# Graph attention and a graph convolution on one core: the second batch's keys and values as block products, and six scalings ahead of a rectification

## The chip, the core and the metric

The kernel runs on one core of a Trainium2 chip. The metric is device time in microseconds (us), smaller is better. The kernel before took 2423.48 us, the median of three runs (2422.51 to 2423.66).

A core has five engines that run side by side and wait for each other by semaphores: TensorE (PE, matrix products into PSUM; its weight loads are listed as PEld), VectorE (DVE), ScalarE (ACT), GpSimd (POOL) and SyncE (SP, which here issues most DMAs). PSUM holds eight banks of 128 x 512 floats.

## The reference, cut to what matters

x is 16 x 1024 x 256 (batch, node, channel), adj is 1024 x 1024, all in float32. Two layers, each with a residual and a layernorm:

```
# layer 0: attention with graph-mixed queries
fea = x^T;  c_adj = mean over channels
Wg = adj * (1 - |2*sigmoid(c_adj[m]-c_adj[n]) - 1|), symmetrised   # per batch
q  = relu((fea @ Wg) * para)          # 4 heads of 64
k, v = split(x @ kv_w)                # kv_w: 256 x 512
x = layernorm(x + softmax(q k^T * scale) v)
# layer 1: A_hat = normalised adj
h = relu(batchnorm((A_hat @ x) @ W1^T + b1));  o = batchnorm(h @ W2^T + b2)
x = layernorm(x + o)
```

## The kernel before

All of this concerns `fast_path`. Layer 0 works one batch at a time, 16 batches in a row. For a batch b there are 32 *units* (two pairs of heads, two halves of the queries, eight blocks of 128 keys). A unit is a call of `scores` (L1152: keys times queries into a two-bank PSUM tile `ps`, then the exponential on ACT, L1157, into a tile `p`) and a call of `outputs` (L1173: `p` times the values into `po`; DVE adds the `p` of a group into `acc`, L1181 and L1183). There are two `ps` tiles and four `p` tiles. Units are issued in 16 bursts of two, numbered u = 0 to 15: scores of burst u, then outputs of burst u-1.

Between the bursts of batch b, the next batch's preparation and the end of the batch before are threaded in. The order of every instruction on PE, ACT, DVE and SP is written out by hand (`tc.manual_schedule`); an engine takes its instructions strictly in the order of the program text. POOL is left to the order of its calls. The pieces that matter here:

- `prologue(b)` makes the closures of a batch's preparation: `begin` (channel sums on DVE, L812, and the row `crow`), the transposes of x, the weights `wg` (ACT: abs L840 and tanh L845; DVE: times adj, L849), the queries, the keys and values.
- Batch 0's queries are plain products (`graph_first`, L979, then `queries`, L966 and L969). For the other batches q is seven block products of a 2 x 2 blocking with sums of blocks on either side (seven products instead of eight): `p1` to `p7` (L899). p1, p2 and p3 run in burst 4 of the batch before, p6, p7, p5 and p4 in burst 8. p2 ends in DVE's product with para (L930) and ACT's rectification (L909); p3 ends in an ACT copy (L926).
- Keys and values of batches 0 and 1 are plain products: `keys` (L994) and `values` (L1007), four steps each. Batches 2 to 15 have them as seven block products too: `kv_step` for k = 1, 6, 5, 7, 3, 4 in burst 0 of the batch before, and `kv_last` (k = 2) in burst 4, between p1 and p2. Each product has a part for the keys (L1054, 512 columns) and one for the values (L1057, four times 128 columns). DVE prepares four sums of blocks of x (`kv_sum`, L1049) and adds each product in (L1066); ACT copies the first (L1074). POOL prepares sums of the weights once (`kv_weight_sums`, L756 to L759), partly over the weights themselves, so after the last plain product has read them.
- The layernorm of batch b-1 (`moments_x1`, `apply_x1`) is threaded into bursts 2 to 5 of batch b, for b = 1 to 14. ACT takes the sums (L1286, L1290), POOL makes the coefficients (L1296 to L1300), ACT scales the eight blocks of 256 columns (L1305), and behind the eighth it issues the DMA that stores x (L1310). In burst 4 ACT's order is: second moments, four scalings, the rectification of p2, the copy of p3. In burst 5: two exponentials, four scalings, the store. SP then loads the x of batch b+2 into the tile that the store frees (L770), a batch that DVE's channel sums in burst 8 read.

The head of the program prepares batch 0 and then batch 1: `graph_first(0..7)` with pieces of batch 1's weights in between, then batch 1's four `values` and four `keys` steps, then the first scores.

After layer 0 come the graph products of layer 1 (L1733), two linear layers with batchnorm (L1765, L1942) and the last residual and layernorm (L2078 to L2167); nothing of them is touched.

Of the kernel before, what the change touches and what calls it, by code (L numbers as in the profile page):

```python
# [515 lines left out]
def fast_path(  # L516
# [23 lines left out]
    NCH = N // P  # L540
# [184 lines left out]
    graph = ExitStack()  # L725
# [9 lines left out]
    with (  # L735
# [17 lines left out]
        def kv_weight_sums():  # L753
            (a11, a12), (a21, a22) = kvA
            s2, s3, s4 = (kvS[:, i] for i in range(3))
            nc.gpsimd.tensor_tensor(s3, a11, a21, ALU.subtract)  # L756
            nc.gpsimd.tensor_tensor(a21, a21, a22, ALU.add)
            nc.gpsimd.tensor_tensor(s2, a21, a11, ALU.subtract)
            nc.gpsimd.tensor_tensor(s4, a12, s2, ALU.subtract)  # L759

        st = {}

        def load_x(b):
            t = xp.tile([P, NCH, C], F32, tag="x", name=f"x_{b}")
            src = x[b].rearrange("(n p) c -> p n c", p=P)
            if b == 0:
                for n in range(0, NCH, 4):
                    nc.sync.dma_start(t[:, n : n + 4, :], src[:, n : n + 4, :])
            else:
                nc.sync.dma_start(t, src)  # L770
            st[b] = {"x": t}

        def load_squares(b, c):
            xs = st[b]["xS", c] = xsp.tile([P, N // SQ, SQ], F32, tag="xS", name=f"xS_{b}_{c}")
            src = x[b].rearrange("(j k) (c q i) -> c q k j i", k=SQ, q=NQ, i=SQ)
            for q in range(NQ):
                nc.sync.dma_start(xs[q * SQ : (q + 1) * SQ], src[c, q])
# [20 lines left out]
        def prologue(b):  # L798
# [6 lines left out]
            def step(f, *a):  # L805
                steps.append((f, a))
# [212 lines left out]
            kv = {}  # L1019
# [85 lines left out]
            else:  # L1105
                first.append((begin, ()))
                first += [(transpose_squares, (c,)) for c in range(CC)]
            for i in range(4 if b < 2 else 0):
                step(values, i)
                step(keys, i // 2, i % 2)  # L1110
            for n in range(NCH if b == 0 else 0):
# [15 lines left out]
            if b:  # L1127
                s["graph"] = dict(
                    between=between, p=(None, p1, p2, p3, p4, p5, p6, p7), right=right, left_first=left_first,
                    kv=(kv_tiles, kv_sum, kv_step, kv_last), q_tile=q_tile,  # L1130
# [186 lines left out]
        def run(fs, k):  # L1317
            for f, a in fs[:k]:
                f(*a)
            del fs[:k]  # L1320
# [135 lines left out]
        with tc.manual_schedule(  # L1456
# [10 lines left out]
            next_first, next_steps, next_side = prologue(1)  # L1467
            for i in range(8):
# [3 lines left out]
                if i == 6:  # L1472
                    run(next_first, 1)
                    load_squares(1, 0)
            run(side, 99)
            for n in range(NCH):
                run(steps, 1)
                if n in (1, 5):
                    run(next_first, 1)
                if n == 1:  # L1480
                    load_squares(1, 1)
                if n:
                    run(next_side, 3)
            for _ in range(8):
                run(next_steps, 1)
                run(next_side, 1)
            kv_weight_sums()
            full, sums, late = [], [], []
            rows_of = []

            def back(j):

                for i in bursts[j]:
                    outputs(i)
                b, pr, qh, m = units[bursts[j][-1]]
                if m == NCH - 1 and qh == 1:
                    sums.append((normalise, (b, pr)))
                    for q in range(2):
                        full.append((residual, (b, pr, q)))
                    if pr == PAIRS - 1:  # L1500
                        if b < B - 2:
                            lo, hi = range(NCH // 2), range(NCH // 2, NCH)
                            late.extend(
                                [(moments_x1, (b, k, ns)) for k in (1, 2) for ns in (lo, hi)]
                                + [(apply_x1, (b, ns)) for ns in (lo, hi)]
                            )

            last, before_last = {}, {}
# [16 lines left out]
            for i in range(4):  # L1525
                ns = range(2 * i, 2 * i + 2)
# [4 lines left out]
            for j in range(len(bursts)):  # L1531
                b, u = j // PERB, j % PERB
                outputs_first = j and u == 0 and b < B - 1
                if outputs_first:
                    back(j - 1)
                for i in bursts[j]:
                    scores(i)
                if u == 0:
                    steps, side = next_steps, next_side
                    next_first, next_steps, next_side = [], [], []  # L1540
                if j and not outputs_first:
                    back(j - 1)
                if outputs_first:
                    run(sums, 1)
                if u in (5, 9, 13):
                    run(rows_of, 1)
                if u == 5:
                    run(late, 1)
                if u == 5 and b + 2 < B:
                    load_x(b + 2)  # L1550
                    next_first, next_steps, next_side = prologue(b + 2)
                if b == B - 1:
                    if u == 0:
                        run(sums, 1)
                        run(rows_of, 1)
                    elif u in (2, 13):
                        run(full, 2)
                    elif u == 8:
                        run(sums, 1)
                    elif u == 3:  # L1560
                        late.clear()
                elif u == 0:
                    if b == 0:
                        run(rows_of, 1)
                        run(side, 99)
                    else:
                        tiles, total, product, kv_last = st[b + 1]["graph"]["kv"]
                        tiles()
                        total(2)
                        for i, k in enumerate((1, 6, 5, 7, 3, 4)):  # L1570
                            if i == 0:
                                run(side, 1)
                            product(k, 0)
                            product(k, 1)
                            if i == 0:
                                run(rows_of, 1)
                                run(side, 1)
                                total(3)
                            run(side, (1, 2, 2, 2, 1, 0)[i])
                            if i == 2:  # L1580
                                total(4)
                elif u < 4:
                    if u == 1:
                        run(full, 2)
                    run(side, (None, 1, 2, 3)[u])
                    if u == 3:
                        st[b + 1]["graph"]["left_first"]()
                    if u > 1:
                        run(late, 1)
                elif u == 4:  # L1590
                    gr = st[b + 1]["graph"]
                    p = gr["p"]
                    run(late, 1)
                    p[1]()
                    if b:
                        run(kv_last(), 2)
                    gr["right"](1)
                    run(late, 2)
                    p[2]()
                    p[3]()  # L1600
                elif u == 8:
                    gr = st[b + 1]["graph"]
                    p = gr["p"]
                    p[6]()
                    run(next_first, 1)
                    run(sums, 1)
                    if b == B - 2:
                        adjacency_diagonal()
                        for n in range(6):
                            adjacency_rows(n)  # L1610
                    p[7]()
                    gr["right"](4)
                    p[5]()
                    p[4]()
                elif u < 8:
                    st[b + 1]["graph"]["between"](u)
                else:
                    if u == 9 and b + 2 < B:
                        load_squares(b + 2, 0)
                    if u == 11:  # L1620
                        run(full, 2)
                    if u == 12:
                        run(next_first, 1)
                        if b + 2 < B:
                            load_squares(b + 2, 1)
                    if u == 15:
                        run(next_first, 1)
                    run(next_side, 2 if u == 11 else 1)
                    if u == 14 and b + 2 < B:
                        st[b + 2]["graph"]["kv"][1](1)  # L1630
                if b == B - 2:
                    run(before_last.get(u, []), 9)
                if b == B - 1:
                    run(last.get(u, []), 9)
# [603 lines left out]
```

## Time and profile before

| what | value |
|---|---|
| median of three runs | 2423.48 us |
| the profiled execution | 2424.15 us |
| its span, first to last instruction | 2422.4 us |
| granted TensorE clock, mean | 0.996 |
| first scores of batch 0 | 65.6 us |
| one batch of layer 0, batches 1 to 14 | some 95.4 us |
| busy in one such batch: PE, DVE, ACT, POOL | 94.8, 87.2, 67.1, 11.2 us |
| last scores of layer 0 | 1541 us |

The profile is one execution taken by the hardware profiler. Its page lists the busy time of each engine, and the groups of instructions by line. The list of waits says for each line how long its engine stood still before it, and which instruction released it. The timeline of an engine gives start, duration, line, operation, output <- inputs, shape, and in brackets the idle time just before with its releaser; equal neighbours are merged ("x16" is sixteen records, and the duration covers all of them). A matrix product in float32 leaves two records per operation. The ends of PE's records are modelled, and neighbours overlap in it; so the starts of PE's rows are the better measure.

### The profile page before, as it was taken

The numbers are of one execution on the slowest core, as the hardware profiler recorded it, in microseconds if no ns is written. First come the engines' busy times: TensorE is split into PE (matmuls) and PEld (weight loads), VectorE is DVE, ScalarE is ACT, GpSimd is POOL, SyncE is SP. The second block draws the span as 40 slices with busy tenths as digits, with TensorE's granted clock in tenths as the row PEclk, the third lists the DMA queues.
The fourth block names the chain that finished last, engine by engine and source line by source line (L and its number), as shares of the span: only waits on it lengthen the run. The fifth ranks groups of instructions, "written<-read, shape, count | busy, mean of one in ns | idle before, by whom it ended". The sixth has DMA issues, their size and how long they took to land. (4 is left out here: it accounts for less than half of the span.)

```text
span 2422.4 us, 33863 instructions
## 1 busy us (share of the span) xinstructions
PE 2378.9 (98%) x12602; PEld 1014.3 (42%) x12602; DVE 1924.7 (79%) x2757; ACT 1323.7 (55%) x1931; POOL 358.2 (15%) x429
## 2 busy tenths in 40 slices
PE   9999999999999999999999999999999999999996
PEld 5343443443434434434434343344444444444444
DVE  5698999989989989899899898955454454479878
ACT  7386776866866867768658677411011011045468
POOL 1011011010110110111101102421111111010026
PEclk9999999999999999999999999999999999999998
DMA  5124222232242242332422426232122122165558
GB/s 165 40 41 88 58 49 71 54 71 65 38 88 58 45 86 55 54 71 42 83 61 41 84 49 112 69 105 104 70 87 104 70 87 104 55 236 178 174 199 358
DMA packets 437886, 222.06 MB, mean 92 GB/s; under 512 B 361552, under 2 KB 411216, under 8 KB 431568
## 3 DMA queue, kind: packets, MB, share of 16 engines
q1 hardware_dynamic: 418400, 169.20, 28.3%
q0 software_dynamic: 2528, 33.57, 3.3%
q10 hardware_dynamic: 16784, 17.04, 2.1%
q8 instruction: 101, 1.65, 0.3%
q14 instruction: 73, 0.60, 0.1%
HBM read 136.06 MB, written 83.69 MB: 91 GB/s over the span
## 5 line engine op out<-in xcount | busy, mean ns | idle before, releaser
L1157 ACT ACTIVATE p<-ps 128x1024 f32<-128x1024 f32 x512 | 497.2, 1021 | 114.8 <-PE ps L1152 95.5
L1183 DVE TENSOR_TENSOR acc<-acc,p 128x1024 f32<-128x1024 f32 x384 | 495.6, 1291 | 35.9 <-ACT p L1157 13.7
L1152 PE MATMUL ps<-qT,kT 64*64 64x512 f32 x4096 | 489.6, 593 | 9.2 <-ACT p L1157 9.2
L1173 PE MATMUL po<-p,v 64*64 64x512 f32 x4096 | 482.8, 589 | 0.0
L1173 PEld LDWEIGHTS po<-p,v 64*64 64x64 f32 x4096 | 158.2, 133 | 281.2 <-issue 278.2
L1152 PEld LDWEIGHTS ps<-qT,kT 64*64 64x64 f32 x4096 | 147.4, 132 | 301.0 <-issue 202.0
L1259 POOL TENSOR_TENSOR o<-o,r_all 128x512 f32<-128x512 f32 x34 | 65.7, 1949 | 638.1 <-DVE r_all L1243 597.2
L849 DVE SCALAR_TENSOR_TENSOR wg<-wg,adj_s 128x1024 f32<-128x1024 f32 x128 | 151.4, 1214 | 3.8 <-ACT wg L845 3.8
L840 ACT ACTIVATE wg<-crow,ccol 128x1024 f32<-128x1024 f32 x128 | 146.4, 1144 | 0.1
L845 ACT ACTIVATE wg<-wg 128x1024 f32<-128x1024 f32 x128 | 135.6, 1060 | 2.2
L909 ACT ACTIVATE qT<-qT 128x512 f32<-128x512 f32 x60 | 37.4, 630 | 168.8 <-DVE qT L912 145.3
L648 DVE SCALAR_TENSOR_TENSOR u_h<-b_h,col_b,p_h 128x512 f32<-128x512 f32 x60 | 45.1, 751 | 98.7 <-PE b_h L1765 98.7
L899 PE MATMUL pgb<-wg,S 128*128 128x512 f32 x240 | 111.0, 605 | 0.0
L899 PE MATMUL pga<-wg,x 128*128 128x512 f32 x240 | 109.6, 599 | 0.7 <-ACT qT L921 0.7
L1733 PE MATMUL a_agg<-ahT,x1l 128*128 128x512 f32 x240 | 108.1, 593 | 0.7 <-ACT agg L1444 0.7
L1733 PE MATMUL b_agg<-aT,x1S 128*128 128x512 f32 x240 | 107.9, 592 | 0.0
L656 ACT COPY p_h<-a_h 128x512 f32<-128x512 f32 x30 | 17.6, 585 | 164.6 <-PE a_h L1765 163.5
L669 ACT ACTIVATE hw<-a_h,col_b 128x512 f32<-128x512 f32 x30 | 20.6, 687 | 132.0 <-PE a_h L1765 132.0
L656 ACT COPY p_agg<-a_agg 128x512 f32<-128x512 f32 x15 | 8.8, 586 | 141.7 <-PE a_agg L1733 141.7
L1296 POOL TENSOR_SCALAR mm_l<-mm_l 128x4 f32<-128x4 f32 x28 | 12.2, 435 | 490.6 <-ACT qT L1286 490.6
L1181 DVE TENSOR_TENSOR acc<-p,p 128x1024 f32<-128x1024 f32 x64 | 77.4, 1210 | 7.5 <-ACT p L1157 7.5
L1305 ACT ACTIVATE x<-x,mm_l 128x256 f32<-128x256 f32 x112 | 58.0, 595 | 44.6 <-POOL mm_l L1300 44.6
(286 smaller groups left out, 3897.9 us busy)
## 6 DMA issues: line engine op xcount, KB each, us to landing
h<-hw POOLq DMA_DIRECT2D x16, 2048.0 KB, 6.6
hl<-h SPq DMA_DIRECT2D x32, 1024.0 KB
x<-x ACTq DMA_DIRECT2D x16, 1024.0 KB
x1l<-x SPq DMA_DIRECT2D x16, 1024.0 KB
xf<-x SPq DMA_DIRECT2D x16, 1024.0 KB
o<-oS SPq DMA_DIRECT2D x62, 256.0 KB
o<-o SPq DMA_DIRECT2D x248, 64.0 KB
x<-in_x_dram SPq DMA_DIRECT2D x15, 1024.0 KB
```

What stands on the lines that cost most here:

```text
L840: nc.scalar.activation(w, s["crow"], AF.Abs, bias=s["ccol"][:, n : n + 1])
L845: nc.scalar.activation(w, w, AF.Tanh, scale=0.5)
L849: nc.vector.scalar_tensor_tensor(w, w, 1.0, adj_s[:, n, :], op0=ALU.subtract, op1=ALU.mult)
L899: nc.tensor.matmul(ps, left, right, start=(start and i == 0), stop=(i == NCH // 2 - 1), skip_group_check=True,)
L1152: nc.tensor.matmul(ps[kh * D : (kh + 1) * D, hd * HALF : (hd + 1) * HALF], kT[r, pr, ks], qT[r, pr, qh * HALF : (qh + 1) * HALF], start=Tr ...
L1157: nc.scalar.activation(p, ps, AF.Exp)
L1173: nc.tensor.matmul(g["po"][kh][hd * D : (hd + 1) * D, :], s["v"][r, m, h * D : (h + 1) * D], p[r, hd * HALF : (hd + 1) * HALF], start=(m = ...
L1181: nc.vector.tensor_add(g["acc"], g.pop("p0"), p)
L1183: nc.vector.tensor_add(g["acc"], g["acc"], p)
L1259: nc.gpsimd.tensor_tensor(oh, oh, r, ALU.mult)
L1305: nc.scalar.activation(s["x"][:, n, :], s["x"][:, n, :], AF.Identity, bias=s["mm"][:, 3, n : n + 1], scale=s["mm"][:, 2, n : n + 1],)
L1733: nc.tensor.matmul(ps, left, right, start=(start and i == 0), stop=(i == NCH // 2 - 1), skip_group_check=True,)
```

## The change

It has two edits.

First, batch 1's keys and values become seven block products as well. In the head, the weight sums are called before batch 0's graph products instead of after batch 1's keys and values. The first two sums of blocks of x go behind batch 1's second transpose, and six products, with the other two sums and what remains of batch 1's weights between them, stand where the eight steps of keys and values stood. The seventh product goes into burst 4 of batch 0, as it does in the other batches.

Second, the eight scalings of a layernorm are divided six and two instead of four and four: six in burst 4, ahead of p2's rectification, and two in burst 5, behind the exponentials.

```
-            for i in range(4 if b < 2 else 0):
+            for i in range(0 if b else 4):
                 step(values, i)
                 step(keys, i // 2, i % 2)
...
             run(side, 99)
+            kv_weight_sums()
+            tiles, total, product, kv_last = st[1]["graph"]["kv"]
             for n in range(NCH):
                 run(steps, 1)
                 if n in (1, 5):
                     run(next_first, 1)
+                if n == 5:
+                    total(1)
+                    total(2)
                 if n == 1:
                     load_squares(1, 1)
                 if n:
                     run(next_side, 3)
-            for _ in range(8):
-                run(next_steps, 1)
+            tiles()
+            for k in (1, 6, 5, 7, 3, 4):
+                product(k, 0)
+                product(k, 1)
+                if k == 1:
+                    total(3)
+                elif k == 5:
+                    total(4)
                 run(next_side, 1)
-            kv_weight_sums()
             full, sums, late = [], [], []
...
                             late.extend(
                                 [(moments_x1, (b, k, ns)) for k in (1, 2) for ns in (lo, hi)]
-                                + [(apply_x1, (b, ns)) for ns in (lo, hi)]
+                                + [(apply_x1, (b, ns)) for ns in (range(6), range(6, NCH))]
                             )
...
                 elif u == 4:
                     gr = st[b + 1]["graph"]
-                    p = gr["p"]
+                    p, kv_last = gr["p"], gr["kv"][3]
                     run(late, 1)
                     p[1]()
-                    if b:
-                        run(kv_last(), 2)
+                    run(kv_last(), 2)
                     gr["right"](1)
                     run(late, 2)
                     p[2]()
```

In the code `total` is `kv_sum`, `product` is `kv_step` with its second argument 0 for keys and 1 for values, and `run(fs, k)` calls the next k closures of a list.

More of the change, by code (lines that the diff above doesn't have):

```diff
@@ L1107, in prologue @@
                 first += [(transpose_squares, (c,)) for c in range(CC)]
-            for i in range(4 if b < 2 else 0):
+            for i in range(0 if b else 4):
                 step(values, i)
@@ L1475, in fast_path @@
             run(side, 99)
+            kv_weight_sums()
+            tiles, total, product, kv_last = st[1]["graph"]["kv"]
             for n in range(NCH):
@@ L1479, in fast_path @@
                     run(next_first, 1)
+                if n == 5:
+                    total(1)
+                    total(2)
                 if n == 1:
@@ L1483, in fast_path @@
                     run(next_side, 3)
-            for _ in range(8):
-                run(next_steps, 1)
+            tiles()
+            for k in (1, 6, 5, 7, 3, 4):
+                product(k, 0)
+                product(k, 1)
+                if k == 1:
+                    total(3)
+                elif k == 5:
+                    total(4)
                 run(next_side, 1)
-            kv_weight_sums()
             full, sums, late = [], [], []
@@ L1504, in back @@
                                 [(moments_x1, (b, k, ns)) for k in (1, 2) for ns in (lo, hi)]
-                                + [(apply_x1, (b, ns)) for ns in (lo, hi)]
+                                + [(apply_x1, (b, ns)) for ns in (range(6), range(6, NCH))]
                             )
@@ L1591, in fast_path @@
                     gr = st[b + 1]["graph"]
-                    p = gr["p"]
+                    p, kv_last = gr["p"], gr["kv"][3]
                     run(late, 1)
                     p[1]()
-                    if b:
-                        run(kv_last(), 2)
+                    run(kv_last(), 2)
                     gr["right"](1)
```

## The prediction

> **What bounds the kernel now.** The page's first part comes first: how full is each engine?
>
> ```profile
> PE 2378.9 (98%) x12602; PEld 1014.3 (42%) x12602; DVE 1924.7 (79%) x2757; ACT 1323.7 (55%) x1931; POOL 358.2 (15%) x429
> ```
>
> PE is busy for 98% of the span, so the time falls only where PE has less to issue or stops waiting. The list of waits, cut to PE, says where it waits. The columns are total us, times, longest:
>
> ```profile
> PE ps L1152 <- ACT p L1157: 9.2, 15, 0.7
> PE pf L2078 <- DVE xf L2106: 7.7, 13, 0.7
> PE pxT L826 <- DMA x<-in_x_dram: 5.0, 1, 5.0
> ```
>
> The first row lies in the attention stage: scores wait until an exponential has read their PSUM tile. The change works there. Batches 1 to 14 have one such wait each, 0.58 to 0.66 us, always in the eighth burst (u = 7); the fifteenth, 0.28, is at the start. Now the timeline of PE in batch 6, from burst 5 on:
>
> ```profile
> 760.44 1.95 PE L1152 MATMUL ps<-qT,kT 64*64 64x512 f32 x16
> 762.21 1.90 PE L1173 MATMUL po<-p,v 64*64 64x512 f32 x16
> 763.92 1.90 PE L1152 MATMUL ps<-qT,kT 64*64 64x512 f32 x16
> 765.64 1.90 PE L1173 MATMUL po<-p,v 64*64 64x512 f32 x16
> 768.20 2.00 PE L1152 MATMUL ps<-qT,kT 64*64 64x512 f32 x16 [0.66 <-ACT p L1157]
> 770.02 1.90 PE L1173 MATMUL po<-p,v 64*64 64x512 f32 x16
> ```
>
> Starts are 1.72 us apart except around the wait, where 2.56 and 1.82 stand. From the first row to the next product p6 (775.28) it is 14.84 us. Batch 0 has no layernorm before it and needs 13.90 for the same stretch (93.23 to 107.13). The wait thus costs 0.94 us, not the 0.66 in brackets. ACT in the same window tells why:
>
> ```profile
> 758.29 2.08 ACT L1305 ACTIVATE x<-x,mm_l 128x256 f32<-128x256 f32 x4 [3.19 <-POOL mm_l L1300]
> 761.73 0.63 ACT L909 ACTIVATE qT<-qT 128x512 f32<-128x512 f32 x1 [1.36 <-DVE qT L930]
> 762.27 0.57 ACT L926 COPY qT<-pgd 128x512 f32<-128x512 f32 x1
> 762.73 1.94 ACT L1157 ACTIVATE p<-ps 128x1024 f32<-128x1024 f32 x2
> 764.55 2.07 ACT L1305 ACTIVATE x<-x,mm_l 128x256 f32<-128x256 f32 x4
> 766.65 0.37 ACTq L1310 DMA_DIRECT2D x<-x  x1
> 767.12 1.94 ACT L1157 ACTIVATE p<-ps 128x1024 f32<-128x1024 f32 x2 [0.50 <-ACT x L1305]
> ```
>
> Four scalings run ahead of q's rectification (L909), and then ACT idles 1.36 us for DVE's product (L930). Four more run behind the exponentials of burst 5, then the store's issue, and only then the exponentials of burst 6. The first of those ends at 768.14, and PE starts at 768.20.
>
> **The scalings, part by part.** Four scalings take 2.08 us at 0.595 each, so starts are 0.495 apart. Six from 758.29 end at 758.29 + 2.08 + 0.99 = 761.36. L930 runs 761.01 to 761.70, so the two added ones fit into the idle 1.36 with 0.34 to spare, and rectification, copy and exponentials keep their places. That idle time is 1.35 or 1.36 in all 14 batches. The cover is ACT's idle time alone; without it (further down) PE's margin is 0.17, since the first exponential of burst 5 ends at 763.75 and scores need its tile at 763.92.
>
> Behind the exponentials 0.99 goes. The store issues at 765.66 and the exponentials start at 767.12 - 0.99 = 766.13; the first ends at 767.15 and frees PE at 767.21. PE wants the tile at 765.64 + 1.72 = 767.36, the second tile at 768.22 against 768.13. The wait disappears, with 0.15 and 0.09 to spare.
>
> What is late next? DVE, without a pause from burst 1 on, idles 1.42 before p6's sum in burst 8 (1.07 in one batch, with 0.46 just before it); it keeps 0.5 if PE comes 0.94 earlier. The four p buffers: the second exponential of burst 8 would wait some 0.1 for DVE's sum, with nothing close behind it. The load of x issued behind the store (771.52 on SP's queue) moves 0.99 earlier too, its reader 0.94. So the whole 0.94 should be kept. Batches 1 to 3 lose 0.89 each, the other eleven 0.94: 2.7 + 10.3 = **13.0 us less**.
>
> **Second batch's keys and values.** Today four value and four key steps stand ahead of the first scores, 32 full-width records of 0.43: 51.58 (first pv) to 65.61 (first scores) is 14.03. PE's rows of batch 6 give the replacement:
>
> ```profile
> 751.73 1.02 PE L1054 MATMUL kve<-xT,kvw_s 128*128 128x512 f32 x2
> 752.59 1.05 PE L1057 MATMUL kve<-kvw_s,xT 128*128 128x128 f32 x8
> 753.48 3.60 PE L899 MATMUL pga<-wg,x 128*128 128x512 f32 x8
> ...
> 819.06 1.12 PE L1054 MATMUL kva<-xT,kvw_s 128*128 128x512 f32 x2
> ```
>
> One product for keys and values is 0.86 + 0.89 = 1.75. Six in a row, as in u = 0 of batch 6, last 10.71 (819.06 to 829.77). Ahead of the first scores that would be 3.3 less. DVE won't allow it. Its order there becomes: four rectification products, wg, a sum, two adds, wg, two adds, a sum, wg, six adds. Durations: adds and sums 0.69 (starts 0.6 apart), wg 1.22. The first add waits for ACT's copy of the first product, behind a tanh and an abs (54.06 + 1.17): copy done 55.78. From there: adds 55.84 and 56.44, wg to 58.26, adds to 59.5, sum to 60.1, wg to 61.2, product 7's adds 61.8 and 62.4, product 3's 63.0 and 63.6. PE must wait for product 5's add before accumulating product 3 (58.7 becomes 58.96) and for product 7's before product 4 (60.7 becomes 61.86). It then ends at 63.6; first scores at 63.7, **1.9 less**. Bounds: 3.3 less where DVE keeps up; 0.4 less where its chain is 1.5 longer. I take 1.9, from the rows.
>
> The seventh product goes into burst 4 of batch 0, between p1 and p2. There p2 now waits 0.68 for ACT's copy (p1 81.79, p2 86.17: 4.38). With a product between, as in batch 6, it is 3.54 + 1.75 = 5.29: **0.9 more**. Its two adds on DVE lie before L930, which idles 3.56.
>
> POOL's three weight sums (0.72 each) come from 65 to about 23.5 to 26, beside DVE's csum reduction (2.28) that the second wg waits for, and that PE waits for. The nearest rows are at odds: two sums L1183 beside POOL took 4.05 instead of 2.55, a transpose L1202 beside POOL's L1260 0.71 as ever. At the first ratio the reduction grows 1.3. I take 0, because it has a single SBUF input like the transpose and the slowed sum has two; 1.3 stays as an end. The two sums put ahead of the queries delay DVE from 50.06 to about 50.15: 0.1. Net of this part: -1.9 + 0.9 = **-1.0**, from -2.4 to +1.8 (0.4 less, 0.9 and 1.3 more).
>
> The Trainium skill's page "TensorE: Matmul & The Clock Gate" (section "Back-to-back issue gap") speaks against block products: in a stream of weight loads and 128-column matmuls it gives about 81 ns each, against about 56 isolated. As an estimate from that ratio, 1.46 x 0.86 would make a value half 1.25, +0.4 each, +2.7 for seven, and the time 2412.2. The trace disagrees, 0.89 for the eight 128-column records against 0.86 for two of 512 columns, and decides.
>
> **Sum.** The profiled execution took 2424.15 (span 2422.4 and 1.75 around it): 2424.15 - 13.0 - 1.0 = 2410.2. The three runs' median, 2423.48, is 0.67 lower: **2409.5 us**.
>
> **Rivals.**
> - Part of the wait stays or turns up elsewhere: margins are 0.09 to 0.15 at the scores and 0.5 at DVE. If half survives: 2423.48 - 6.5 - 1.0 = 2416.0. For it: thin margins. Against: they hold in all 14 batches. Chance 0.16.
> - No gain: DVE, pause-free from burst 1 to 8, is the real bound, or the wait has another cause. 2422.5. Against: DVE idles 1.42 before p6's sum, and PE starts 0.06 after the exponential's end. Chance 0.08.
> - Slower: the six scalings hold up the rectification. If they end d later than L930, the exponentials, scores and all behind them are d late. The 0.94 goes, and each batch is slower than before from about d = 0.85 on, that is 0.34 + 0.85 = 1.2 us above my row. At d = 1.6, 14 x 0.75 - 1.0 gives 2433. Even unoverlapped scalings (0.595 apart) reach only d = 0.26. Chance 0.03.
> - Weight loads bound the 128-column products, 1.25 for a value half: 14.0 - 2.7 saved, 2412.2. The rows refute it: chance 0.01.
>
> The forecast has the remaining 0.72, at 2407 to 2412. The range reaches through half of the first rival: **2406.5 to 2416.5**. Faster by over 0.2% (4.8 us, about what a measurement here can tell from none): 0.72 + 0.16 + 0.01 = 0.89; within it 0.08; slower 0.03.
>
> **What would show it.** PE's list of waits: ps on ACT falls from 15 times and 9.2 us to one or two. ACT: L1305 as six, then two, with L909 still released by DVE's L930 some 0.35 after the sixth. Burst 5 to p6 is 13.9 in batches 1 to 14, the batch 94.5 instead of 95.4. First scores near 63.7, and p1 to p2 in batch 0 5.3. I am wrong if L909 comes right behind the sixth scaling, if PE waits at burst 6's scores, or if DVE's idle time before p6's sum is gone and PE waits for DVE.

## The result, and the profile after

The changed kernel takes 2409.16 us, the median of four runs (2409.01 to 2409.73), against 2423.57 for the kernel before (four runs, 2422.51 to 2423.85). The ratio is 0.9942, with a 95% interval of 0.9925 to 0.9959: 14.4 us less, where 14.0 was forecast. The profiled execution took 2409.73 with a span of 2407.9, 14.5 less than before.

The page's line of busy times, which answers to the first one shown of before:

```profile
PE 2372.7 (99%) x12624; PEld 1015.8 (42%) x12624; DVE 1932.6 (80%) x2771; ACT 1322.4 (55%) x1927; POOL 358.9 (15%) x429
```

PE is busy 6.2 us less in a span that is 14.5 shorter. The rest is time in which it stood still. Not all of the 6.2 is work saved, either: each wait before has 0.28 us that the profile counts as busy (last section), 3.9 us in 14 batches. The waits of PE (total us, times, longest), cut to those that answer to before and the two new ones in the head:

```profile
PE pf L2087 <- DVE xf L2115: 7.7, 13, 0.7
PE pxT L826 <- DMA x<-in_x_dram: 5.0, 1, 5.0
...
PE kvd L1054 <- DVE kT L1066: 0.9, 1, 0.9
...
PE kvc L1054 <- DVE kT L1066: 0.4, 1, 0.4
PE ps L1152 <- ACT p L1157: 0.3, 1, 0.3
```

Scores on exponentials have gone from 15 waits and 9.2 us to one of 0.3, the one at the start. The two waits of block products on DVE's adds are those that the prediction worked out for the head.

First, a label. With batches counted from 0, the stretch at 760 us that the prediction and the expectations call batch 6 lies in batch 7: its wait is the seventh of the fourteen, and the first is batch 1's. The six products at 819 us lie in burst 0 of batch 8. The stretch is called batch 7 from here on. PE in batch 7, from burst 5 on (start, duration, line):

```profile
754.49 1.04 PE L1152 MATMUL ps<-qT,kT 64*64 64x512 f32 x8
755.35 1.90 PE L1173 MATMUL po<-p,v 64*64 64x512 f32 x16
757.07 1.90 PE L1152 MATMUL ps<-qT,kT 64*64 64x512 f32 x16
758.79 1.90 PE L1173 MATMUL po<-p,v 64*64 64x512 f32 x16
760.50 1.90 PE L1152 MATMUL ps<-qT,kT 64*64 64x512 f32 x16
762.22 1.90 PE L1173 MATMUL po<-p,v 64*64 64x512 f32 x16
```

(The first row is the second half of a burst that the window cuts.) From outputs to scores to outputs it is 1.71 or 1.72 throughout; the 2.56 and 1.82 of before are gone. From one batch's p6 to the next one's it is 94.5 us (767.48 to 862.00), before 95.5 (775.28 to 870.74). ACT in the same batch:

```profile
751.43 3.06 ACT L1305 ACTIVATE x<-x,mm_l 128x256 f32<-128x256 f32 x6 [3.18 <-POOL mm_l L1300]
754.87 0.63 ACT L909 ACTIVATE qT<-qT 128x512 f32<-128x512 f32 x1 [0.38 <-DVE qT L930]
755.40 0.57 ACT L926 COPY qT<-pgd 128x512 f32<-128x512 f32 x1
755.87 1.94 ACT L1157 ACTIVATE p<-ps 128x1024 f32<-128x1024 f32 x2
757.69 1.09 ACT L1305 ACTIVATE x<-x,mm_l 128x256 f32<-128x256 f32 x2
758.81 0.37 ACTq L1310 DMA_DIRECT2D x<-x  x1
759.28 1.94 ACT L1157 ACTIVATE p<-ps 128x1024 f32<-128x1024 f32 x2 [0.50 <-PE ps L1152]
761.61 1.94 ACT L1157 ACTIVATE p<-ps 128x1024 f32<-128x1024 f32 x2 [0.39 <-PE ps L1152]
```

The six scalings eat 0.98 of the 1.36 that ACT used to wait for DVE; 0.38 is left, and the rectification L909 is still released by DVE's L930. DVE's idle time before p6's sum, in the kernel before and now:

```profile
779.02 0.69 DVE L944 TENSOR_TENSOR qT<-pgb,qT 128x512 f32<-128x512 f32 x1 [1.42 <-PE pgb L899]
```

```profile
771.22 0.69 DVE L944 TENSOR_TENSOR qT<-pgb,qT 128x512 f32<-128x512 f32 x1 [0.49 <-PE pgb L899]
```

In the head, the same view of PE as before, from the first block product to the first scores:

```profile
51.16 1.02 PE L1054 MATMUL kva<-xT,kvw_s 128*128 128x512 f32 x2
...
58.68 1.10 PE L1054 MATMUL kvc<-xT,kvS 128*128 128x512 f32 x2 [0.35 <-DVE kT L1066]
59.61 1.05 PE L1057 MATMUL kvc<-kvS,xT 128*128 128x128 f32 x8
61.52 1.12 PE L1054 MATMUL kvd<-xT,kvw_s 128*128 128x512 f32 x2 [0.85 <-DVE kT L1066]
62.48 1.05 PE L1057 MATMUL kvd<-kvw_s,xT 128*128 128x128 f32 x8
63.47 1.95 PE L1152 MATMUL ps<-qT,kT 64*64 64x512 f32 x16
```

That is 12.31 us, against 14.03 for the eight plain steps: 1.72 less. From p1 to p2 in batch 0 it is 5.29 (79.65 to 84.94), before 4.38: 0.91 more. Net 0.8 in this execution.

The first product also starts 0.42 earlier than in the profile before. The edit has no part in that: the first step of batch 0's values takes 2.18 here (8.60 to 10.78) and 2.71 in the profile before, and it varies between executions of the same head (2.75 in the one with seven scalings further down). The early start costs part of the gain. DVE's second transpose waits for x to land and starts only 0.19 earlier than before (45.15 instead of 45.34), so DVE's chain does not come forward with PE: its rectification products L966 (49.88) stand behind its own work without idle time, while with seven and one they wait 0.37 for PE. PE then waits longer for DVE's adds. In four other executions with the same head (five and three, seven and one, eight and none, and the changed kernel with added DVE work, all below) the first product starts at 51.7 to 52.2, and the stretch to the first scores is 12.08, 1.95 less than before; in the one of the block products alone it starts at 51.03 and the stretch is 12.67.

### The profile page after: what moved, and what is told of

It is laid out like the page before. It is cut to its first block, busy times and chain, and to the rows that moved or that the text cites. A ratio compares the mean times of both kernels' runs of the same rounds, so it can differ in the third digit from the quotient of the medians.

```text
span 2407.9 us, 33928 instructions
## 1 busy us (share of the span) xinstructions
PE 2372.7 (99%) x12624; PEld 1015.8 (42%) x12624; DVE 1932.6 (80%) x2771; ACT 1322.4 (55%) x1927; POOL 358.9 (15%) x429
## 4 chain that ended last, share of the span: by engine, by line
PE 94%; DVE 3%; DMA 1%; ACT 1%; issue 0%; SPq 0%; POOL 0%; DVEq 0%; POOLq 0%; ACTq 0%
PE ps L1152 19%; PE po L1173 18%; PE pgb L899 7%; PE b_agg L1742 6%; PE pga L899 4%; PE a_agg L1742 4%; PE c_agg L1742 4%; PE b_h L1774 3%; PE b_o L1951 3%; PE c_h L1774 2%; PE pgc L899 2%; PE pgd L899 2%; PE a_h L1774 2%; PE a_o L1951 2%; PE c_o L1951 2%; PE den L1221 1%
## 5 line engine op out<-in xcount | busy, mean ns | idle before, releaser
L1183 DVE TENSOR_TENSOR acc<-acc,p 128x1024 f32<-128x1024 f32 x384 | 495.4, 1290 | 35.4 <-ACT p L1157 13.6
L1259 POOL TENSOR_TENSOR o<-o,r_all 128x512 f32<-128x512 f32 x34 | 65.6, 1948 | 665.8 <-DVE r_all L1243 625.8
L849 DVE SCALAR_TENSOR_TENSOR wg<-wg,adj_s 128x1024 f32<-128x1024 f32 x128 | 151.3, 1213 | 2.6 <-ACT wg L845 2.6
L909 ACT ACTIVATE qT<-qT 128x512 f32<-128x512 f32 x60 | 37.4, 630 | 156.1 <-DVE qT L912 145.3
L1854 ACT ACTIVATE hl<-hl,bn_sh,bn_sg 128x1024 f32<-128x1024 f32 x64 | 75.7, 1232 | 8.6 <-DMA hl<-h 5.9
```

The costliest lines, as they stand in the source:

```text
L849: nc.vector.scalar_tensor_tensor(w, w, 1.0, adj_s[:, n, :], op0=ALU.subtract, op1=ALU.mult)
L1183: nc.vector.tensor_add(g["acc"], g["acc"], p)
L1854: nc.scalar.activation(h, h, AF.Relu, bias=sh1[:, k : k + 1], scale=sg1[:, k : k + 1])
```

## The experiments

The runs set the prediction's theory against these rivals: the gain comes from the block products, or from the store's place rather than from the number of scalings; DVE is the real bound; scalings ahead of the rectification hold it up.

**Each part alone.** The first kernel is the kernel before with one line changed, the second the changed kernel with that line as before:

```
-                                + [(apply_x1, (b, ns)) for ns in (lo, hi)]
+                                + [(apply_x1, (b, ns)) for ns in (range(6), range(6, NCH))]
```

> The kernel before with the scalings six and two, keys and values of the second batch as before. If the waits before burst 7's scores were what the scalings are worth (0.89 in three batches, 0.94 in eleven), 2423.5 - 13.0 = 2410.5, and PE's list of waits has ps on ACT once, 0.3. If the gain came mostly from the block products, 2422 or more.

> The changed kernel with the scalings four and four again, so only the block products of the second batch. Head and burst 4 of batch 0 together: 1.72 less from the first product to the first scores, 0.91 more between p1 and p2, so 2423.5 - 0.9 = 2422.6, with 14 waits of 0.6 before burst 7's scores. If products were bound by weight loads it would be 2424 or more.

Six and two alone: 2410.62 (2409.42 to 2411.29), ratio 0.9945, interval 0.9929 to 0.9962. Block products alone: 2422.36 (2421.0 to 2423.24), ratio 0.9994, interval 0.9985 to 1.0004, beside 2423.46 for the kernel before. So 12.8 and 1.1, together 13.9, and with both edits 14.4: the parts add up to within the scatter, and the scalings are nine tenths of it. The 1.1 alone can't be told from none by its interval. That it is a gain rests on the traces: 0.91 more in burst 4, and 1.36 to 1.95 less ahead of the first scores in six executions with that head. In the second kernel ps on ACT still has its 15 waits and 9.3 us, in the first it has one of 0.3.

**How many scalings.** The same line with other divisions, in the changed kernel (the lines are cut to the part that differs, and the comments are added here).

```
-  for ns in (range(6), range(6, NCH))
+  for ns in (range(5), range(5, NCH))        # five and three
+  for ns in (range(7), range(7, NCH))        # seven and one
+  for ns in (range(NCH),)                    # eight, the store ahead too
```

> The changed kernel with five scalings ahead and three behind. By the chain of the waits, the first exponential of burst 6 ends 0.495 later than with six and two, at 767.65 in the counting of batch 6 of the kernel before, and frees PE at 767.71 instead of the wanted 767.36: a loss of 0.35 and about 0.1 for the restart, 14 x 0.45 = 6.3, so 2415.5. If any shift of scalings out of burst 5 freed the tile early enough (the wait being only the store's issue), 2409.2.

> Seven scalings ahead, one behind. Seven end at 761.86 in the counting of batch 6 before, 0.13 past the end of DVE's product L930, so the rectification is some 0.1 late and follows the scalings instead of DVE. PE's margin before burst 6's scores is 0.17, so nothing is lost: 2409.2, within 1. If the 0.34 spare behind the sixth scaling was the last cover, 0.13 + 0.1 per batch, 2412.4.

> All eight scalings and the store's issue ahead of the rectification, none behind the exponentials. Eight end 1.98 later than four, at 762.35 in the counting of batch 6 before, and the store's issue takes 0.5 more: the rectification starts at about 762.85 instead of 761.73, 1.12 late. The exponentials of burst 5 are as late, burst 6's scores wait 1.0 and lose 1.1 per batch: 2409.2 + 14 x 1.1 = 2424.6, the kernel before or slightly slower, with PE waiting for ACT before burst 6's scores instead of burst 7's. If ACT's order ahead of the rectification does not reach PE, 2409.

Measured: five and three 2415.54 (interval of the ratio 0.9956 to 0.9978), seven and one 2409.24 (0.9925 to 0.9959), eight and none 2423.37 (0.9990 to 1.0010). With the change's six and two at 2409.16 and its four and four at 2422.36, the time falls by 6.8 and 6.4 for the fifth and the sixth scaling, not at all for the seventh, and rises by 14.1 for the eighth with the store. The wait of five and three, in PE's timeline:

```profile
761.69 1.90 PE L1173 MATMUL po<-p,v 64*64 64x512 f32 x16
763.76 2.00 PE L1152 MATMUL ps<-qT,kT 64*64 64x512 f32 x16 [0.17 <-ACT p L1157]
765.58 1.90 PE L1173 MATMUL po<-p,v 64*64 64x512 f32 x16
```

Starts are 2.07 and 1.82 apart instead of 1.72 twice: 0.45 lost, as expected, behind an idle time of only 0.17. The list of waits has it for 11 of the 14 batches. Batches 1 to 3 show no idle time at that place, and still take 0.4 longer from p6 to p6 than in the changed kernel (94.94, 94.91 and 94.92 against 94.53). The store's issue is directly behind the last scaling with four, five, six and seven ahead, while the time differs by 13 us; so the number of scalings ahead of the exponentials decides, not the store. With eight and none the wait has moved by a burst. ACT and, in the second view, PE:

```profile
758.21 4.04 ACT L1305 ACTIVATE x<-x,mm_l 128x256 f32<-128x256 f32 x8 [3.19 <-POOL mm_l L1300]
762.28 0.37 ACTq L1310 DMA_DIRECT2D x<-x  x1
762.70 0.63 ACT L909 ACTIVATE qT<-qT 128x512 f32<-128x512 f32 x1 [0.44 <-ACT x L1305]
```

```profile
762.13 1.90 PE L1173 MATMUL po<-p,v 64*64 64x512 f32 x16
764.78 2.00 PE L1152 MATMUL ps<-qT,kT 64*64 64x512 f32 x16 [0.75 <-ACT p L1157]
766.60 1.90 PE L1173 MATMUL po<-p,v 64*64 64x512 f32 x16
```

The rectification follows ACT's own work instead of DVE, and PE waits before burst 6's scores: 2.65 and 1.82 instead of 1.72 twice, 1.03 per batch. The expected 1.1 was 0.1 too much, and the time 1.2. This is the slower rival of the prediction, made to happen: its mechanism is real, but it takes two more scalings and the store to reach it, and even then the kernel only comes out even with the one before.

Seven and one, on ACT:

```profile
751.76 3.56 ACT L1305 ACTIVATE x<-x,mm_l 128x256 f32<-128x256 f32 x7 [3.18 <-POOL mm_l L1300]
755.22 0.62 ACT L909 ACTIVATE qT<-qT 128x512 f32<-128x512 f32 x1
```

Its rectification follows the seventh scaling directly, with no idle time. But it is hardly late: it starts 3.46 behind the first scaling, against 3.44 with six (and 3.44 with four), because its row begins 0.10 before the end of the scaling's. The exponentials of burst 5 start 4.44 behind the first scaling in both. So the 0.1 of lateness that was expected didn't come, and PE's margin of 0.17 wasn't put to the test.

**Is DVE the bound?** `left_third`, one DVE difference of about 0.6 us whose result is written again unchanged, done three times in burst 7, once in the kernel before and once in the changed one:

```
                 if u == 7:
                     left_third()
+                    left_third()
+                    left_third()
```

> The kernel before with left_third, a DVE difference of 0.6 us, done three times instead of once in burst 7 (the same values are written again). If PE and ACT set the time there and DVE has 1.42 us to spare before p6's sum, the added 1.2 is hidden: 2423.5. If DVE were the real bound of the batch, 15 x 1.2 = 18 more, 2441.

> The same two added differences in the changed kernel, where DVE idles only 0.49 before p6's sum. The added 1.2 makes that sum 0.7 late, and p7, which accumulates on the same bank, waits for it: 0.6 and 0.1 for the restart in 14 batches, nothing in batch 0 (1.56 idle): 2409.2 + 9.8 = 2419. If DVE still had the 1.42 of the kernel before, 2409; if it were the bound throughout, 2427.

Before: 2424.25 (2422.92 to 2425.04), interval of the ratio 0.9993 to 1.0012, beside 2423.58. After: 2420.08 (2419.4 to 2421.14), 10.9 more than without them. The same work costs 0.7 in one kernel, within its interval (up to 2.9), and 10.9 in the other. DVE in batch 7 of the kernel before, with the additions:

```profile
778.58 0.71 DVE L1204 STREAM_TRANSPOSE oS<-oT 128x512 f32<-128x512 f32 x1
779.26 0.69 DVE L946 TENSOR_TENSOR qT<-pgb,qT 128x512 f32<-128x512 f32 x1
```

There is no idle time before p6's sum any more (L946 in this kernel's numbering), and PE does not notice: from p6 to p7 it takes 4.63 (775.52 to 780.15), as in the kernel before. In the changed kernel it does. The row in PE's list of waits, and p7 in batch 7:

```profile
PE pgb L899 <- DVE qT L946: 8.8, 14, 0.6
```

```profile
778.10 3.70 PE L899 MATMUL pgb<-wg,S 128*128 128x512 f32 x8 [0.64 <-DVE qT L946]
```

From p6 to p7 it is now 5.34 (772.76 to 778.10), 0.71 more: the added 1.2 less the 0.49 of idle time. Over 14 batches that is about the 9.8 that was expected; where the other 1.1 of the 10.9 comes from is open. So DVE was not the bound, but after the change it is 0.49 us away from being it; work that was free before is paid for now.

**A better version.** In the changed kernel's head PE waits 0.35 and 0.85 for DVE. Two of the products of the weights with adj (L849) leave the head for burst 0 of batch 0:

```
                 if k == 1:
                     total(3)
+                    run(next_side, 1)
                 elif k == 5:
                     total(4)
-                run(next_side, 1)
```

> The changed kernel with the last two products of the second batch's weights with adj (L849, 1.2 us each on DVE) taken from between the block products in the head to burst 0 of batch 0, where DVE idles 2.1. If DVE's chain holds PE there (waits of 0.35 and 0.85 before products 3 and 4), both waits go: first scores 1.4 earlier, 2407.8. If the wait for ACT's copy of the first product sets the chain, 2409.

2407.34 (2406.95 to 2408.01), ratio 0.9934, interval 0.9917 to 0.9951. Its four runs lie below all four of the changed kernel. PE's row of the first scores, and DVE's of the moved products:

```profile
61.80 1.95 PE L1152 MATMUL ps<-qT,kT 64*64 64x512 f32 x16
```

```profile
62.69 2.36 DVE L849 SCALAR_TENSOR_TENSOR wg<-wg,adj_s 128x1024 f32<-128x1024 f32 x2
64.95 1.23 DVE L1181 TENSOR_TENSOR acc<-p,p 128x1024 f32<-128x1024 f32 x1
```

From the first product (51.01) to the first scores it is 10.79, against 10.71 for the same six products in a full batch, 12.31 in the changed kernel's trace and 12.08 in the four others with its head. Both waits are gone from PE's list. The moved products run where DVE used to idle 2.1 us for the first exponentials. It is the fastest of all versions here.

## Why the prediction was right

- **What bounds the kernel.** PE, with the waits for ACT as what the change can take away: right. Two more differences on DVE in each batch of the kernel before cost nothing that can be told from the scatter.
- **The price of a wait.** Taken as 0.94 from the starts of PE's rows, not as the 0.66 in brackets. From batch 0's p6 to batch 14's it is 1336.53 us before (107.13 to 1443.66) and 1323.36 after (105.79 to 1429.15): 13.2 less in 14 batches, 0.94 each. The 0.66 would have given 9.2.
- **The cover.** Two scalings in ACT's 1.36 of idle time with 0.34 to spare: 0.38 were spare. The time with seven scalings also came out as expected, but not on PE's margin: the rectification was 0.02 late and not 0.1.
- **What is late next.** DVE was to keep 0.5 of its 1.42: 0.49. The second exponential of burst 8 was to wait some 0.1 for DVE's sum: it waits 0.30 by the bracket and is 0.4 late by the starts (1.33 behind the first instead of some 0.91). The size was wrong, but nothing behind it on PE is late.
- **The block products.** First scores at 63.7, with products 3 and 4 held up by 0.3 and 1.2: 63.47, with 0.35 and 0.85 in brackets, 0.52 and 1.02 by the starts. The head gave 1.72 in this execution and not 1.9, because PE came early and DVE's chain did not; where the head started as late as in the profile before or later, it gave 1.95. The 0.9 in burst 4 was 0.91. Net 0.8 in this trace, 1.0 in four others, 1.1 by the kernel with that part alone, against 1.0.
- **POOL's weight sums at no cost.** Of the two rows that were at odds the right one was chosen. DVE's reduction took 2.28 beside them, as ever. What did grow was POOL's first sum over the weights (last section), which nothing but POOL's own next sums waited for.
- **Weight loads.** The value halves of the products take 0.89 in the head where no wait follows, as in the other batches, not 1.25.
- **Slips that changed nothing.** Six scalings 0.595 apart would end at 758.29 + 3.57 = 761.86, 0.16 behind L930's end, and not d = 0.26. And the slower rival was priced a little too high: eight scalings and the store made the rectification 1.05 late (4.49 behind the first scaling instead of 3.44) at a cost of 1.03, so a batch breaks even with the wait of before (0.94) some 0.1 later than at the d = 0.85 given (an estimate from that one point).

The forecast of 2409.5 against 2409.16 also has luck in it: the scalings alone gave 0.2 less than forecast, the block products 0.1 more, and both together 0.4 more, all within the scatter of single runs (about 1 us).

## What to carry to other kernels

When one engine is busy throughout, look for its short waits that come back in every round, and price them by the starts of its rows against a round that has none; the bracketed idle time was too small by up to 0.28 us here, and a short wait can be missing from the list. Work on another engine that stands ahead of what the bound engine waits for belongs into the other engine's own idle time, and the profile gives the room in it as a number: here it held two more scalings with 0.38 left, a third with nothing left, and not a fourth with the store. Each such move eats slack elsewhere, so note what is left of it, because the next change will be made against that.

## What the runs showed of the hardware

A wait of PE costs more than its idle time in the profile. At the scores, 0.17 idle cost 0.45, 0.66 cost 0.94, 0.75 cost 1.03, each time 0.28 more. About 0.1 of it is the longer first burst behind the wait (1.82 to the next start instead of 1.72), and 0.18 the modelled end of the row before, which overlaps the next start where nothing waits (1.90 long, 1.72 apart). The 0.28 belongs to these rows and is no constant: 0.64 idle before p7 cost only 0.71. The row before it, of `den` (L1221), is 1.06 long, and p7 follows 1.00 behind its start where nothing waits; p5 starts 3.53 behind p7 with and without the wait.

POOL's first sum over the weights (L757) took 1.44 us in the changed kernel and 0.72 in the kernel before:

```profile
22.29 1.44 POOL L757 TENSOR_TENSOR kvw_s<-kvw_s 128x256 f32<-128x256 f32 x1 [13.28 <-PE pk L994]
23.80 0.73 POOL L758 TENSOR_TENSOR kvS<-kvw_s 128x256 f32<-128x256 f32 x1
24.62 0.73 POOL L759 TENSOR_TENSOR kvS<-kvw_s,kvS 128x256 f32<-128x256 f32 x1
```

It began while DVE ran a product of two SBUF operands (L849, 21.92 to 23.14), and the other two ran beside DVE's reduction of one operand (L812, from 23.05, 2.28 long) with neither slowed. The Trainium skill's page "SBUF — State Buffer" (section "Who interferes with whom") says just that: a VectorE instruction with two SBUF inputs and a GpSimd one that reads SBUF exclude each other, whoever starts first, and a reduction never takes part. The three rows agree. The other order stands in the view of the kernel before: two sums on DVE (L1183, from 800.14) that began while a POOL product ran (L1259, from 799.14) took 4.05 instead of 2.55.
